# Attention in a four-stage kernel: scores of the next pair and values of the last pair alternate on the matmul engine

## The chip, the cores and the metric

The kernel runs on one core of a Trainium2 chip. A core has a matmul engine (PE, with its weight loads shown apart as PEld), three engines for other arithmetic (DVE, ACT, POOL), a queue that issues transfers (SP), and 16 DMA engines that all of them share. Each engine works through its own instructions in the order in which they were written; engines wait for each other by semaphores. The metric is the device time of one execution in microseconds (us), and what is compared are medians of several runs.

## The reference, cut to what matters

The model has four residual stages on `x` (32 sequences of 56 rows of 256), with `ctx` (32 x 1500 x 256) and a mask over the 1500 context rows. The change touches the third:

```python
x = x + _L0_xattn_ref(_layernorm(x), ctx, ...)      # a scan over ctx, summed
x = x + _L0_ffn_ref(_layernorm(x), ...)             # 16 experts, 6 of them a row
x = x + _L1_xattn_ref(_layernorm(x), ctx, mask)     # attention: the stage that is changed
x = x + _L1_ffn_ref(_layernorm(x), ...)             # 2 experts, the better one a row

def _L1_xattn_ref(hidden_states, memory_tokens, memory_mask):
    scale = 1.0 / jnp.sqrt(jnp.asarray(D, hidden_states.dtype))
    scores = jnp.einsum('bsd,bmd->bsm', hidden_states, memory_tokens) * scale
    scores = jnp.where(memory_mask[:, None, :], scores, -1e30)
    attn = jax.nn.softmax(scores, axis=-1)
    readout = jnp.einsum('bsm,bmd->bsd', attn, memory_tokens)
    return jnp.where(jnp.any(memory_mask, axis=-1)[:, None, None], readout, 0)
```

The context rows are keys and values at once. All is float32.

## The kernel before, in words

Two sequences make a **pair**: 16 pairs (`NP`), each 2 x 64 partitions of which 2 x 56 are real rows. `xr` holds the residual of all pairs in SBUF. The order of PE, DVE, ACT, SP and (in the attention stage) POOL is the order of the program text: `manual_schedule` keeps it, so "before" and "after" in the text are so on each engine's queue.

The attention loop runs `p` from 0 to 16. For each pair the work is:

- **Context.** A sequence's context is one slot of 128 x 12 x 256 float32 (1536 KB). There are 8 slots, five in `ring` and three `extra`; `load_ctx` (L145, SP) fills one. A pair's two slots are filled again, with the pair that comes four later, right after its values have been read (end of `attend`).
- **Keys turned.** `turn(p, n)` transposes half `n` of both sequences' contexts on DVE (`transposed`, L908, two instructions a half) into `cT`, four buffers: two halves of two sequences.
- **Scores.** `scores` (L947, PE, `sp`) goes over eight steps `e`, two sequences `h` and four strips `a`: 64 matmuls in the program, which the chip runs as 128 (each float32 matmul is two). Each uses 32 rows and 64 columns of the array, eight such tiles side by side. The four `sp` banks of PSUM have one buffer each.
- **Mask and softmax.** `masked` (L960, DVE) adds the mask terms `mf` and takes the maximum, from `sp` into `sc` (one buffer); `softmax` makes the bias `nb` (L970, DVE) and the exponentials in place (L972, ACT). `mask_added` (L930, ACT) writes `mf` for the next pair from `mu`, which `mask_terms` (L917, SP) loads.
- **Probabilities turned.** `turned` (L987, PE, and copies on ACT, L988) makes `pT`.
- **Values.** `attend` (L995, PE, `op`) sums 12 chunks for two sequences: 24 matmuls, 48 on the chip, each 128 rows by 64 columns, two side by side.
- **After that** `inverse` and `sort_rows` (L1029, DVE) scale and add the residual into `pay`; `stats1`, `roots`, `sort_norm`, `sort_gate` normalise the row and pick its expert; every fourth pair `sort_four`, `sort_rank` (PE, L1063) and `sort_place` compute where four pairs' rows go, and POOL scatters them to `xs1` in DRAM (L1086).
- **For a later pair:** `query_rows` (ACT, L735) and `queries` (PE, L754) prepare the queries of pair `p + 2`, and POOL gathers the second stage's results for pair `p + 5` (`results`, six gathers, L709) and adds them to `xr` (`added`, L719 to L722). This goes on to `p` = 10.

In iteration `p` PE's order is: scores of `p`, values of `p - 1` (held from the last iteration), queries of `p + 2`, a rank if there is one, probabilities of `p` turned. The softmax of `p` runs while PE does the values of `p - 1`. In the last iterations `order_of_blocks` (L1102, a small matmul) and `rows_of1` (L1133, POOL) start the fourth stage for the first `NY1` blocks; the weights of that stage (L1211, L1215, SP) go into `ring` slots 0 to 3, which the contexts of pairs 12 and 13 leave last. The fourth stage is `expert_blocks`: for each block of 128 rows `gate_up` (L647), `turn` and `down` (L674).

Of the kernel before, what the change touches and what calls it, by code (L numbers as in the profile page):

```python
# [8 lines left out]
F32 = mybir.dt.float32  # L9
# [9 lines left out]
P = 128  # L19
B, S, D, T = 32, 56, 256, 1500  # L20
KD = D // P
NP = B // 2
TOK = 2 * S
NM, JM = 3, 4
NCH = NM * JM
# [8 lines left out]
NQ1 = 4  # L34
# [6 lines left out]
NPG = E0 * CAP // P // 2  # L41
NL = CAP // P
NB0 = (B * S * K0 + E0 * (P - 1)) // P
NY1 = 3
NB1 = B * S // P + 1
WP = 2 * D + 2
EPS = 1e-5
# [7 lines left out]
def xattn_ffn_kernel(  # L55
# [23 lines left out]
    V, A, PE, G = nc.vector, nc.scalar, nc.tensor, nc.gpsimd  # L79
# [62 lines left out]
    slots = [ring[:, i, :].rearrange("p (j d) -> p j d", d=D) for i in range(NRING)]  # L142
# [62 lines left out]
    with tc.tile_pool(name="p1", bufs=1) as p1, tc.tile_pool(name="p3", bufs=3) as p3, tc.tile_pool(  # L205
        name="xn", bufs=4
    ) as xnp, tc.tile_pool(name="z", bufs=4) as zp, tc.tile_pool(name="p1_ps", bufs=6, space=PSUM) as ps, tc.tile_pool(
        name="p1_acc", bufs=2, space=PSUM
# [122 lines left out]
        for e in range(KD):  # L331
            PE.matmul(
                vp[:, 0:D], lhsT=bcol[:, e : e + 1].to_broadcast([P, P]), rhs=wout_sb[:, e, :],
                start=(e == 0), stop=False,
# [124 lines left out]
        def turned(p):  # L459
            keep(p, xT=turned_rows(p3, ps, "ps", pend[p]["xn"]))  # L460
# [419 lines left out]


    so = ctx.enter_context(tc.tile_pool(name="so", bufs=1))
    payp = ctx.enter_context(tc.tile_pool(name="pay", bufs=7))
    with tc.manual_schedule(
        engines={ET.PE, ET.DVE, ET.Activation, ET.SP, ET.Pool}
    ), tc.tile_pool(name="at", bufs=1) as at, tc.tile_pool(
# [27 lines left out]
        def mask_terms(p):  # L914

            mu = mus[p % 2]
            nc.sync.dma_start(  # L917
                out=mu, in_=bass.AP(mask.tensor, 2 * p * T, [[T, 2], [0, 64], [1, T]])
            )
            return mu  # L920
# [17 lines left out]
                AF.Identity, scale=BIG, bias=nbig,  # L938
            )

        def scores(cTs, xq):

            sps = [psc.tile([P, 512], F32, tag=f"sp{a}", name=f"sp{a}") for a in range(4)]
            for e in range(NE):
                for h in range(2):
                    for a in range(4):
                        PE.matmul(  # L947
                            sps[a][64 * h : 64 * h + 64, 0 : Q * NCH],
                            lhsT=xq[Q * a : Q * a + Q, e, 64 * h : 64 * h + 64],
                            rhs=cTs[e // 4][h][Q * a : Q * a + Q, :, e % 4, :],  # L950
                            start=(e == 0), stop=(e == NE - 1),
                        )
            return sps

        def masked(sps):
            sc = at.tile([P, NCH, P], F32, tag="sc", name="sc")
            mx = small.tile([P, 5], F32, tag="mx", name="mx")
            for a in range(4):
                cols = (slice(None), slice(None), slice(Q * a, Q * a + Q))
                V.tensor_tensor_reduce(  # L960
                    out=sc[cols], in0=sps[a][:, 0 : Q * NCH].rearrange("p (j q) -> p j q", q=Q),
                    in1=mf[cols], scale=1.0,
                    scalar=-3.0e38, op0=ALU.add, op1=ALU.max, accum_out=mx[:, a : a + 1],
                )
            V.tensor_reduce(mx[:, 4:5], mx[:, 0:4], AX.X, ALU.max)
            return sc, mx

        def softmax(sc, mx):
            nb = small.tile([P, 3], F32, tag="nb", name="nb")
            V.tensor_scalar(nb[:, 0:1], mx[:, 4:5], -ISC, None, ALU.mult)  # L970
            sf = sc.rearrange("p j q -> p (j q)")
            A.activation(sf, sf, AF.Exp, bias=nb[:, 0:1], scale=ISC, accum_out=nb[:, 1:2])  # L972
            return nb
# [14 lines left out]
                A.copy(pT[:, 4 * n : 4 * n + 4, :].rearrange("p j c -> p (j c)"), tp)  # L988
            return pT

        def attend(p, pT):
            op = po.tile([P, 512], F32, tag="op", name="op")
            for j in range(NCH):
                for h in range(2):
                    PE.matmul(  # L995
                        op[64 * h : 64 * h + 64, 0:D],
                        lhsT=pT[:, j, 64 * h : 64 * h + 64],
                        rhs=slots[(2 * p + h) % NS][:, j, :],
                        start=(j == 0), stop=(j == NCH - 1),
                    )  # L1000
            for b in (2 * p + NS, 2 * p + 1 + NS):
                if b < B:
                    load_ctx(b, slots[b % NS])
            return op


        GP = 4
# [19 lines left out]
        def sort_rows(p, op, nb):  # L1027
            pay[p] = payp.tile([P, WP], F32, tag="pay", name="pay")
            V.scalar_tensor_tensor(  # L1029
                pay[p][:, D : 2 * D], op[:, 0:D], nb[:, 2:3], xr[:, p, :], ALU.mult, ALU.add  # L1030
            )
            return stats1(pay[p][:, D : 2 * D])
# [107 lines left out]
        def turn(p, n):  # L1140
            return [transposed(2 * p + h, n) for h in range(2)]
# [5 lines left out]
        def results_until(p):  # L1147
            while sent[0] < due[min(p, NP - 1)]:
                results(*queue[sent[0]])
                sent[0] += 1  # L1150

        cTs = [turn(0, 0), turn(0, 1)]
        mask_added(mu_.pop(0))
        mvs, four = {}, []
        held = None
        for p in range(NP + 1):
            if p == NP - 1:
                order_of_blocks()

            if p + 2 < NP:  # L1160
                roots(mvq[p + 2])
            if p - 2 in mvs:
                roots(mvs[p - 2])
            if p + 2 < NP:
                xn = query_rows(p + 2, mvq.pop(p + 2))
                mu_[p + 2] = mask_terms(p + 2)
            if p - 2 in mvs:
                sort_norm(p - 2, mvs.pop(p - 2))
            if p < NP:
                sps = scores(cTs, xqs.pop(p))  # L1170
                if p + 1 < NP:
                    lo = turn(p + 1, 0)
                sc, mx = masked(sps)
                nb = softmax(sc, mx)
                if p + 1 < NP:
                    cTs = [lo, turn(p + 1, 1)]
                inverse(mx, nb)
            if held:
                op = attend(held[0], held[1])
                mvs[held[0]] = sort_rows(held[0], op, held[2])  # L1180
                held = None
            if NE0 <= p + NE0 < NP:
                added(p + NE0, [results(resp, p + NE0, NB0, i) for i in range(2)])
            if p + 3 < NP:
                mvq[p + 3] = stats1(xr[:, p + 3, :])
            if p + 2 < NP:
                xqs[p + 2] = queries(at2, ppt, "pt", xn, 0)
                queries(at2, ppt, "pt", xn, 1, xqs[p + 2])
            if four:
                sort_place(*four[0], sort_rank(four.pop()[1], ppt, "pt"))  # L1190
            if 0 <= p - 2 < NP:
                sort_gate(p - 2)
                if (p - 2) % GP == GP - 1:
                    o = p - 2 - GP + 1
                    four.append((o, sort_four(o)))
            if p < NP:
                held = (p, turned(sc), nb)
            if p + 1 < NP:
                mask_added(mu_.pop(p + 1))
            if p == NP - 1:  # L1200
                for i in range(NY1):
                    apart()
                    rows_of1(i, payp, "pay")
# [15 lines left out]
    with tc.tile_pool(name="f1", bufs=3) as wk, tc.tile_pool(  # L1219
        name="f1_tr", bufs=2, space=PSUM  # L1220
    ) as ptr, tc.tile_pool(name="f1_gu", bufs=2, space=PSUM) as pgu, tc.tile_pool(
        name="f1_ht", bufs=2, space=PSUM
    ) as pht, tc.tile_pool(name="f1_y", bufs=2, space=PSUM) as py:
        last = NP - GP

        def side1(t):

            if t == -1:
                roots(mvs[NP - 1])
                sort_norm(NP - 1, mvs.pop(NP - 1))  # L1230
                sort_gate(NP - 1)
                four.append((last, sort_four(last)))
            if t == 1:
                sort_place(*four[0], sort_rank(four.pop()[1], ptr, "tr"))
            if t == 2:
                experts_of_rest(ptr, "tr")
            i = t // NQ1 + 2
            if t % NQ1 == 1 and i >= NY1 and i < NB1:
                rows_of1(i, wk, "xb1")

        def done1(i, y):
            xb = xb1.pop(i)
            ti = wk.tile([P, 1], I32, tag="ti", name="ti")
            V.tensor_copy(ti, xb[:, WP - 1 : WP])
            ob = wk.tile([P, D], F32, tag="ob", name="ob")
            V.scalar_tensor_tensor(  # L1246
                ob, y[:, 0:D], xb[:, 2 * D : 2 * D + 1], xb[:, D : 2 * D], ALU.mult, ALU.add
            )
            loose("out", G.indirect_dma_start(  # L1249
                out=of, out_offset=bass.IndirectOffsetOnAxis(ap=ti[:, 0:1], axis=0),  # L1250
                in_=ob, in_offset=None, bounds_check=B * S - 1, oob_is_err=False,
            ))

        expert_blocks(
            NB1, NQ1, F1, w1_sb.rearrange("p e w -> p (e w)"), e1i,
            wk, ptr, pgu, pht, py, lambda i: xb1[i][:, 0:D], done1, 1, None, side1,
        )

# [55 lines left out]
```

## Time and profile before

| | us |
|---|---|
| median of 3 runs (lowest, highest) | 1027.94 (1022.82, 1030.45) |
| the profiled execution's own time | 1017.45 |
| its span, first to last instruction | 1015.7 |
| granted PE clock, mean | 0.882 |
| PE / PEld / DVE / ACT / POOL busy | 878.1 / 551.9 / 460.7 / 348.3 / 419.1 |
| attention stage (first scores to the fourth stage's first matmul) | 547.6 to 833.7 |

All times inside the execution count from the span's start. PE's busy time is no measure of its load: matmuls are pipelined, and the ends of matmuls are modelled. So the stage is read from the start of one group to the start of the next. In the tables of stretches each row has the stretch, its length, and for each engine its busy time with the number of instructions in brackets, then the granted PE clock (1.00 is full), the busy share of the DMA engines and the rate in GB/s. In the chain of waits and in the timeline each row has start, length, engine, line and what is written; in the timeline the bracket at the end is the engine's idle time just before, and what ended it ("issue": nothing that the profile shows).

### The profile page before, as it was taken

Reading aid. Unit: us, or ns where it says so; the run is one execution under the profiler, and the core shown is the slowest. Engines: PE = TensorE matmul, PEld = TensorE weight load, DVE = VectorE, ACT = ScalarE, POOL = GpSimd, SP = SyncE. Lnnn points to the kernel's source line nnn. Section 1 sums busy time; section 2 is a strip of 40 time slices with the busy share of each in tenths; the row PEclk is TensorE's granted clock in tenths of the full one; section 3 lists DMA queues with packets and bytes.
Section 4 is the critical chain, followed back from the end, with each engine's and each line's share of the span. In section 5 each row is a group of like instructions: output and inputs, shape, how many; then the busy total and the mean of one; then the engine's idle time right before and its main releaser. Section 6 shows DMA issues by size and latency. Waiting matters only on the chain.

```text
span 1015.7 us, 17756 instructions
## 1 busy us (share of the span) xinstructions
PE 878.1 (86%) x6122; PEld 551.9 (54%) x6122; DVE 460.7 (45%) x1447; ACT 348.3 (34%) x904; POOL 419.1 (41%) x487
## 2 busy tenths in 40 slices
PE   5687897761698989898898899899999999999997
PEld 4344443331476767676675456555556555666664
DVE  2565454534255323232225657655668933332332
ACT  0222221210242454543333464453466632111111
POOL 4155554544435555555542645644640023021111
PEclk9767655765799999999989799998899999999999
DMA  9999999999397633343435475675575472011110
GB/s 274 364 259 244 231 249 231 279 220 177 93 321 259 196 114 110 112 116 104 125 87 155 169 289 190 237 265 182 181 294 217 146 247 73 11 37 38 31 31 16
DMA packets 81145, 177.08 MB, mean 174 GB/s; under 512 B 10899, under 2 KB 44580, under 8 KB 81060
## 3 DMA queue, kind: packets, MB, share of 16 engines
q1 hardware_dynamic: 64884, 139.78, 45.3%
q0 software_dynamic: 16048, 35.95, 12.8%
q8 instruction: 52, 0.85, 0.4%
q14 instruction: 33, 0.27, 0.1%
q10 hardware_dynamic: 128, 0.23, 0.1%
HBM read 151.06 MB, written 25.53 MB: 174 GB/s over the span
## 4 chain that ended last, share of the span: by engine, by line
PE 64%; issue 6%; DMA 5%; DVE 3%; ACT 2%; another core or an unknown queue 1%; POOL 1%; ACTq 0%; SPq 0%; POOLq 0%; DVEq 0%
PE gu L647 20%; PE sp L947 13%; PE y L674 12%; PE op L995 8%; PE tp L665 3%; DMA ring<-in_cx 3%; PE tp L166 2%; PE tp L987 2%; PE tp L754 1%; DMA own<-pw,to 1%; DVE cT L908 1%; DMA w_sb<-in_wd 1%; ACT xT L168 0%; ACTq L787 0%
## 5 line engine op out<-in xcount | busy, mean ns | idle before, releaser
L647 PE MATMUL gu<-w_sb,xT 128*128 x396 | 139.6, 476 | 21.3 <-ACT xT L168 17.3
L947 PE MATMUL sp<-cT,xq 32*64 32x384 f32 x2048 | 141.5, 544 | 14.1 <-issue 10.6
L779 POOL DMA_INDIRECT xb<-xn,idx x99 | 94.7, 956 | 113.4 <-PE tp L166 89.6
L516 POOL DMA_INDIRECT own<-pw,to x96 | 95.8, 998 | 106.8 <-issue 94.9
L653 ACT ACTIVATE sg<-gu 128x176 f32<-128x176 f32 (+1 forms) x159 | 54.4, 343 | 219.6 <-PE gu L647 209.3
L659 DVE SCALAR_TENSOR_TENSOR hs<-sg,wgt,gu 128x176 f32<-128x176 f32 x99 | 39.3, 397 | 187.5 <-ACT sg L653 178.7
L647 PE MATMUL gu<-ring,xT 128*128 x240 | 114.3, 600 | 0.5 <-ACT xT L168 0.5
L947 PEld LDWEIGHTS sp<-cT,xq 32*64 32x64 f32 x2048 | 70.8, 147 | 76.3 <-issue 61.9
L709 POOL DMA_INDIRECT g<-ys,back x96 | 92.0, 958 | 34.4 <-issue 27.4
L647 PEld LDWEIGHTS gu<-w_sb,xT 128*128 128x128 f32 x396 | 75.4, 194 | 52.8 <-ACT xT L168 19.9
L674 PE MATMUL y<-w_sb,hT 88*128 x396 | 102.4, 381 | 0.0
L294 PE MATMUL acc<-ring,cz 128*32 128x256 f32 x768 | 79.1, 567 | 20.1 <-DMA ring<-in_cx 15.8
L908 DVE STREAM_TRANSPOSE cT<-ring 128x1536 f32<-128x1536 f32 x40 | 69.1, 1759 | 59.3 <-PE sp L947 32.9
L657 DVE TENSOR_TENSOR hs<-sg,gu 128x256 f32<-128x256 f32 x60 | 25.2, 421 | 117.1 <-ACT sg L653 117.1
L665 PEld LDWEIGHTS tp<-ident,hs 128*88 128x88 f32 (+1 forms) x318 | 41.6, 131 | 63.6 <-issue 49.6
L168 ACT COPY xT<-tp 128x256 f32<-128x256 f32 x130 | 48.4, 372 | 79.9 <-PE tp L166 66.1
L674 PEld LDWEIGHTS y<-w_sb,hT 88*128 88x128 f32 x396 | 68.0, 192 | 5.7 <-issue 0.2
L1249 POOL DMA_INDIRECT out<-ob,ti x15 | 15.0, 997 | 132.3 <-DVE ob L1246 121.7
L667 DVE COPY hT<-tp 88x256 f32<-88x256 f32 (+1 forms) x159 | 66.0, 415 | 2.1 <-PE y L674 1.4
L995 PE MATMUL op<-ring,pT 128*64 128x256 f32 x480 | 65.9, 384 | 0.0
L665 PE MATMUL tp<-ident,hs 128*88 128x128 f32 (+1 forms) x318 | 61.8, 277 | 2.6 <-DVE hs L657 2.6
L647 PEld LDWEIGHTS gu<-ring,xT 128*128 128x128 f32 x240 | 45.7, 191 | 33.1 <-issue 29.5
(264 smaller groups left out, 1274.4 us busy)
## 6 DMA issues: line engine op xcount, KB each, us to landing
ring<-in_cx SPq DMA_DIRECT2D x52, 1536.0 KB
extra<-in_cx SPq DMA_DIRECT2D x12, 1536.0 KB
ys<-yb SPq DMA_DIRECT2D x99, 128.0 KB
xs<-zrow SPq DMA_DIRECT2D x5, 771.0 KB
mu<-in_mask SPq DMA_DIRECT2D x16, 187.5 KB
w_sb<-in_wg SPq DMA_DIRECT2D x2, 1408.0 KB
w_sb<-in_wu SPq DMA_DIRECT2D x2, 1408.0 KB
xn<-xn SPq DMA_DIRECT2D x16, 128.0 KB
```

The costliest lines, as they stand in the source:

```text
L294: PE.matmul(acc[Q * g : Q * g + Q, 0:D], lhsT=cz[:, j, 1 - h : 1 - h + Q], rhs=c[:, j, :], start=(h == 0 and m == 0), stop=(h == 1 and m = ...
L516: loose("own", G.indirect_dma_start(out=own, out_offset=bass.IndirectOffsetOnAxis(ap=to[:, k : k + 1], axis=0), in_=pw[:, k, :], in_offset ...
L647: PE.matmul(gu[:, 0 : 2 * fp], lhsT=xT[i][:, k, :], rhs=w[:, bass.ds(at[i] + (u * piece + k * 2 * fp), 2 * fp)], start=(k == 0), stop=(k = ...
L653: A.activation(sg, gu[:, 0:fp], AF.Silu)
L665: PE.transpose(tp[0:h, c * P : (c + 1) * P], a[:, c * h : (c + 1) * h], ident)
L667: V.tensor_copy(hT[i, u], tp[0:h, 0 : 2 * P])
L674: PE.matmul(y[i][:, 0:D], lhsT=a[:, c * P : (c + 1) * P], rhs=w[0:h, bass.ds(at[i] + (u * piece + doff + c * D), D)], start=(u == 0 and c ...
L709: G.indirect_dma_start(out=g[:, k, :], out_offset=None, in_=ys0[0 : n * P, :], in_offset=bass.IndirectOffsetOnAxis(ap=back[:, p, 3 * i + k ...
L779: G.indirect_dma_start(out=xb, out_offset=None, in_=xn0, in_offset=bass.IndirectOffsetOnAxis(ap=idx[:, i : i + 1], axis=0),)
L908: V.transpose(out=cT.rearrange("p j e q -> p j (e q)"), in_=slots[b % NS][:, :, P * n : P * n + P],)
L947: PE.matmul(sps[a][64 * h : 64 * h + 64, 0 : Q * NCH], lhsT=xq[Q * a : Q * a + Q, e, 64 * h : 64 * h + 64], rhs=cTs[e // 4][h][Q * a : Q * ...
L995: PE.matmul(op[64 * h : 64 * h + 64, 0:D], lhsT=pT[:, j, 64 * h : 64 * h + 64], rhs=slots[(2 * p + h) % NS][:, j, :], start=(j == 0), stop ...
```

## The change

The scores go one more pair ahead. Scores and turned keys of pair 1 come before the loop; in iteration `p` PE computes scores of `p + 1` and values of `p - 1`, and the two are generators that `by_turns` takes one piece of each: after each of the eight steps `e` of the scores (8 matmuls in the program) come four or two matmuls of the values, by turns, so eight pieces of each. The probabilities of `p` are turned after that, from exponentials made at the end of the iteration before. `sc` has two buffers. The mask is loaded and added one pair earlier, too. `pay` has six buffers for seven, and two blocks of the fourth stage are fetched early for three; the third is fetched in its step 3.

```diff
-NY1 = 3
+NY1 = 2
...
-    payp = ctx.enter_context(tc.tile_pool(name="pay", bufs=7))
+    payp = ctx.enter_context(tc.tile_pool(name="pay", bufs=6))
...
-        def scores(cTs, xq):
-
-            sps = [psc.tile([P, 512], F32, tag=f"sp{a}", name=f"sp{a}") for a in range(4)]
+        def scores(cTs, xq, sps):
+
+            sps[:] = [psc.tile([P, 512], F32, tag=f"sp{a}", name=f"sp{a}") for a in range(4)]
             for e in range(NE):
...
-            return sps
+                yield
 
         def masked(sps):
-            sc = at.tile([P, NCH, P], F32, tag="sc", name="sc")
+            sc = at.tile([P, NCH, P], F32, tag="sc", bufs=2, name="sc")
...
-        def attend(p, pT):
-            op = po.tile([P, 512], F32, tag="op", name="op")
-            for j in range(NCH):
-                for h in range(2):
-                    PE.matmul(
...
+        def attend(p, pT, op):
+
+            for i in range(2 * NCH):
+                j, h = divmod(i, 2)
+                if i and i % 6 in (0, 4):
+                    yield
+                PE.matmul(
...
             for b in (2 * p + NS, 2 * p + 1 + NS):
                 if b < B:
                     load_ctx(b, slots[b % NS])
-            return op
+            yield
...
+        def by_turns(*parts):
+            parts = list(parts)
+            while parts:
+                parts = [g for g in parts if next(g, g) is not g]
+
         cTs = [turn(0, 0), turn(0, 1)]
         mask_added(mu_.pop(0))
-        mvs, four = {}, []
-        held = None
+        mu_[2] = mask_terms(2)
+        mvs, four, soft, held = {}, [], {}, {}
+        sps = []
+        by_turns(scores(cTs, xqs.pop(0), sps))
+        lo = turn(1, 0)
+        soft[0] = masked(sps)
+        soft[0] += (softmax(*soft[0]),)
+        cTs = [lo, turn(1, 1)]
+        mask_added(mu_.pop(1))
         for p in range(NP + 1):
...
-                mu_[p + 2] = mask_terms(p + 2)
+            if p + 3 < NP:
+                mu_[p + 3] = mask_terms(p + 3)
...
-            if p < NP:
-                sps = scores(cTs, xqs.pop(p))
-                if p + 1 < NP:
-                    lo = turn(p + 1, 0)
-                sc, mx = masked(sps)
-                nb = softmax(sc, mx)
-                if p + 1 < NP:
-                    cTs = [lo, turn(p + 1, 1)]
+
+            parts, sps = [], []
+            if p + 1 < NP:
+                parts.append(scores(cTs, xqs.pop(p + 1), sps))
+            if p >= 1:
+                op = po.tile([P, 512], F32, tag="op", name="op")
+                pT, mx, nb = held.pop(p - 1)
+                parts.append(attend(p - 1, pT, op))
+            by_turns(*parts)
+            if p + 1 < NP:
+                if p + 2 < NP:
+                    lo = turn(p + 2, 0)
+                soft[p + 1] = masked(sps)
+            if p >= 1:
                 inverse(mx, nb)
-            if held:
-                op = attend(held[0], held[1])
-                mvs[held[0]] = sort_rows(held[0], op, held[2])
-                held = None
+                mvs[p - 1] = sort_rows(p - 1, op, nb)
+            if p + 2 < NP:
+                cTs = [lo, turn(p + 2, 1)]
...
             if p < NP:
-                held = (p, turned(sc), nb)
+                sc, mx, nb = soft.pop(p)
+                held[p] = (turned(sc), mx, nb)
             if p + 1 < NP:
-                mask_added(mu_.pop(p + 1))
+                soft[p + 1] += (softmax(*soft[p + 1]),)
+            if p + 2 < NP:
+                mask_added(mu_.pop(p + 2))
...
+            if t == 3:
+                rows_of1(NY1, wk, "xb1")
             i = t // NQ1 + 2
-            if t % NQ1 == 1 and i >= NY1 and i < NB1:
+            if t % NQ1 == 1 and NY1 < i < NB1:
                 rows_of1(i, wk, "xb1")
```

More of the change, by code (lines that the diff above doesn't have):

```diff
@@ L989, in turned @@
             return pT
-        def attend(p, pT):
-            op = po.tile([P, 512], F32, tag="op", name="op")
-            for j in range(NCH):
-                for h in range(2):
[L995 to L1000, printed above, removed]
+        def attend(p, pT, op):
[4 more added lines that the diff above has]
+                PE.matmul(
+                    op[64 * h : 64 * h + 64, 0:D],
+                    lhsT=pT[:, j, 64 * h : 64 * h + 64],
+                    rhs=slots[(2 * p + h) % NS][:, j, :],
+                    start=(j == 0), stop=(j == NCH - 1),
+                )
             for b in (2 * p + NS, 2 * p + 1 + NS):
```

## The prediction, made before the changed kernel was run

> **What bounds the stage now.** I read the chain of waits first. In the late pairs it is PE alone, without a gap:
>
> ```profile
> 771.09 5.35 PE sp L947 x128
> 776.43 5.33 PE op L995 x48
> 781.76 1.03 PE tp L754 x8
> 782.79 1.38 PE tp L987 x12
> 784.17 5.35 PE sp L947 x128
> ```
>
> A pair costs 784.17 - 771.09 = 13.08 us: scores 5.35, values 5.33, small transposes 2.41. 16 pairs would take 210 us; the stage takes 286. The values always take 5.33 at full clock. What varies is the scores. Next I asked for the stretch of each pair's scores with the POOL gathers (L709) in it (columns: stretch, length, busy POOL us with its count, granted clock, DMA share, GB/s):
>
> ```profile
> 585.10:593.30 8.20, 1.96 (x3) 1.00 1.03 396
> 600.90:613.70 12.80, 3.77 (x4) 0.73 0.82 307
> 673.90:692.20 18.30, 5.80 (x6) 0.68 0.72 248
> 701.20:709.00 7.80, 1.66 (x2) 1.00 1.02 391
> 784.10:789.50 5.40, 0.00 (x0) 1.00 1.03 419
> sum 153.20, POOL 35.96; mean POOL 2.25
> ```
>
> The 16 stretches sum to 153.20 us where 16 x 5.40 = 86.4 would do: **66 us lost in the scores**, always where POOL issues gathers (or, for pairs 11 and 15, the scatters of L1086). Busy DMA alone does not do it: the last row has 1.03 and no loss. How it goes shows in stretches that begin where a burst of six gathers begins, and in those that follow (all engines; PE and its loads come first):
>
> ```profile
> 598.30:602.75 4.45, 4.45 (x62) 3.20 (x61) 3.68 (x12) 3.50 (x7) 3.53 (x4) 1.00 0.63 214
> 652.19:657.90 5.71, 5.71 (x67) 3.90 (x64) 5.18 (x16) 1.92 (x5) 4.49 (x5) 1.00 0.54 160
> 714.27:718.90 4.63, 4.63 (x63) 3.25 (x62) 3.14 (x12) 3.89 (x8) 3.71 (x4) 1.00 0.70 237
> ...
> 602.75:606.50 3.75, 2.78 (x12) 0.46 (x5) 0.00 (x0) 3.62 (x11) 2.22 (x3) 0.88 1.04 389
> 657.90:660.60 2.70, 1.26 (x8) 0.37 (x4) 1.04 (x6) 1.44 (x6) 1.26 (x2) 1.00 1.04 419
> ```
>
> From the burst's start PE gets through some 63 matmuls (55 to 70 in seven bursts), whatever they are, and then nearly stops (5 weight loads in 3.75 us) until about 1.2 us after the last gather (658.51 + 0.96, PE at pace again at 660.68). No semaphore is named: the releaser is "issue". So PE has a stock of some 63 matmuls and gets almost none while POOL writes gathers. Values use 24 matmuls (48 on the chip) in 5.33 us, and the stock outlasts the burst; scores use 24 a us, and it is gone in 2.6. A dry spell of 3.6 us or more is followed by half clock (0.73 in the rows above).
>
> ```profile
> 652.19 0.97 POOL L709 DMA_INDIRECT g<-ys,back  x1
> ...
> 658.51 0.96 POOL L709 DMA_INDIRECT g<-ys,back  x1 [0.30 <-issue]
> 665.35 1.83 POOL L719 TENSOR_TENSOR g<-g 128x768 f32<-128x768 f32 x1 [5.88 <-DMA g<-ys,back]
> ```
>
> A burst is 7.3 us long; with the wait for landing (5.9) and the additions (4.3) POOL goes round in some 17.7 us by itself, eleven times.
>
> **Part 1: changes between scores and values on PE.** The work of a pair is the same in number and size. But scores use tiles of 32x64, values of 128x64, and where one follows the other PE pauses:
>
> ```profile
> 775.59 0.85 PE L947 MATMUL sp<-cT,xq 32*64 32x384 f32 x16
> 776.37 0.87 PE L995 MATMUL op<-extra,pT 128*64 128x256 f32 x6
> ```
>
> Single starts: the last scores matmul at 775.954, the first of the values at 776.365, 0.411 us later where one tile's scores follow each other every 0.322; and the first pair of values lies 0.267 apart, later ones 0.2155. Lost: 0.089 + 0.052 = 0.14 us. Probabilities to scores (770.816 to 771.019) gives 0.144 in the same way, values to queries 0.155. Values to scores doesn't occur in this program; I take 0.14, the nearest rows, with 0 and 0.155 as ends. Eight pieces each make 15 changes where there was one, in the 14 iterations that have both (`p` 1 to 14): 14 x 14 x 0.14 = **+27.4 us** (0 to +30.4). Nothing lies beside it, as PE is the chain; nor can it be a gain, as scores and values each ran back to back before and left no gaps to fill. Scores and values of one iteration then take 10.68 + 1.96 = 12.64, a pair 15.05.
>
> The Trainium skill speaks against the change here: "TensorEngine Tiling (Array Packing)", Key Properties, says that changing the tiling mode, not just the tile, drains the engine. It gives no price; had PE overlapped the two modes, this term would be 0.
>
> **Part 2: the bursts.** Interleaved, PE uses 176 matmuls in 12.64 us, 13.9 a us. A burst of 7.3 + 1.2 = 8.5 us finds stock for 63 / 13.9 = 4.5, leaving some 4 dry, of which the trickle seen above gives back 0.5: 3.5 a burst, and as 4 is at the point where half clock followed (3.6 did, 2.7 did not), 0 to 2.5 more. Eight such bursts: 28 to 48. The first (scores of pair 0 are as before) 4.6, the second, over the small transposes, 3 to 4. The long one (four scatters and six gathers on end, 12.5 us; before, 12.9) 10 to 12.4. Four scatters alone, which let through more (19 matmuls in 3.8 us), 1.6, before 4.2. The last scatters meet no scores any more, before 3.6. Sum 47 to 70.6, mean 59, against 66: **-7 us** (-19 to +5).
>
> The skill would have this term at nothing: "Runtime: NRT & Kernel Launch", Instruction fetch mechanics, holds a kernel's instruction stream to be mostly hidden. The rows have PE short of instructions with no wait; where they stay the trace doesn't tell.
>
> **Part 3: the fourth stage's start.** Its weights go to slots that the values of pair 13 leave. These end at 807.87, and DMA stays busy (1.01) until 829, 0.57 to 831, then idle; the sequencer's waits before the first matmul (L647, 833.68) include the last weight load, which landed at 830.5, 22.7 us after. Before, scores of pair 15 (8.9 us) lay in that time, now they come ahead of it: PE is ready 25.8 - 8.9 = 16.9 after. It waits 5.8, or 7.6 with the sequencer's steps from landing to matmul: **+6 us** (0 to +7.6).
>
> **Part 4: small ones.** Before, PE waited 3.6 us in iteration 0 for the first softmax; now 2.3 for `masked` and up to 1 for a half turned: -1 (-3 to +3). In each iteration `masked` of `p + 1` now starts when its scores end, and PE's next scores, with the values queued behind them, wait for its four PSUM banks: 0.16 + 4 x 0.48 + 0.1 = 2.2 us, under 2.41 of small transposes. This covers it by 0.2; without, up to 2 an iteration. DVE then has 8.6 us of rows up to the bias `nb`, ACT 1.8 exponentials and 4.75 from mask to query rows: 15.1 after the values' end, just the new 15.05; with `sort_four` (1.9 on DVE) it is late by 2, in the one late iteration with it: **+2** (0 to +8). The mask's load is queued ahead of the context loads on SP and waits for ACT; that ends some 2 us before the values do. Transposing on DVE (3.43 a half) has 6.3 us of the other half's scores to hide in. `pay` with six buffers makes `sort_rows` wait for the first scatter of a group, an iteration (15 us) older. The third block's gather comes with those that ran at 850 and is needed at 856. Each of these is 0, and some 2 to 4 us once if the cover is gone, inside the ends above.
>
> **Sum:** 27.4 - 7 + 6 - 1 + 2 = +27.4. Against the profiled execution's own 1017.45 that is 1044.9. The median shown lies 10.5 higher, so the forecast for a median is 1027.94 + 27.4 = **1055 us**.
>
> **Rivals.** (a) *The stock lasts (faster).* The turns are there to thin PE's demand. The shortest stretch with a burst in it lost 2.4 us (701.20, 7.80 less 5.4). If each of ten bursts costs that, and the long one 9, scatters 1.6: 35, or -31; changes that fall into dry spells cost nothing, so half of them, 14; with +6 and +1, -10: 1018. If changes are at the low end, 0, it is 1004. It decides from 63 / (7.3 + 1.2 - 2.4) = 10.3 matmuls a us down; the turns need 13.9, which speaks against it. I put it at 1010. (b) *Changes cost little:* 0 to 5, with -7 for bursts and 0 to 7 for the rest: 1021 to 1033, say 1029. For it: weight loads are drawn ahead of matmuls within one shape. Against it: three measured changes agree on 0.14. That the turns don't reach PE at all is not likely, its order being the text's; the time would be this one. (c) *Context loads come late.* A pair's slots are filled after the values of `p - 1` and now turned in the middle of the next iteration, where they had one iteration more. Loads took 12.6 us (582.5 to 595.1) to 13.5 beside gathers, 10.4 to 11 without. With values ending at 12.64, second transpose 1.75 and masks 2.2, twice the period is at least 16.6 + landing: 15.0 at 13.5, not above 15.05. At 17 it is 16.8, 1.75 x 14 = +24.5 on the sum: 1080.
>
> **Numbers.** Forecast 0.55 (1040 to 1070); (a) 0.12; (b) 0.21; (c) 0.12. Range 1024 to 1080: it takes in most of (b), the forecast and half of (c), and leaves out (a). A measurement here tells about 1% from no change. Faster by over 1% (under 1017.7): (a), 0.12. Within 1% (to 1038.2): most of (b), 0.19. Slower: 0.69.
>
> **What would show it.** Late pairs (no POOL gathers) at some 15 us for 13.08, with 0.41 and not 0.32 us between a scores piece and the values after it; stretches of scores and values 12.6 without a burst, 16 to 19 with one; the first L647 later against the end of pair 13's values than 16.9. I am wrong if late pairs stay near 13 (changes are free), if the stretches with bursts stay under 14 (the stock lasts), or if DVE's transposes wait for loads (c).

## The result, and the profile after

| | before | changed |
|---|---|---|
| median (lowest, highest), four runs each | 1025.38 (1019.65, 1030.45) | 1078.7 (1070.36, 1085.61) |
| profiled execution, span | 1015.7 | 1077.7 |
| attention stage, first scores to first matmul of the fourth stage | 286.1 | 337.6 |
| second stage (its first L647 to the first scores), same code in both | 283.6 | 290.6 |

The change makes the kernel slower: ratio 1.0518, 95% interval 1.0421 to 1.0615, 53 us by the medians and 51.5 in the attention stage. The time of the kernel before differs between the batches in which experiments ran together (1025, 944.6, 944.5, 964.0, 1007.0 us), so below each kernel is set against the kernel before in its own batch, and stages against stages.

Stretches of scores and values in the changed kernel, six of the 14 (columns: stretch, length, busy POOL us in gathers with their count, granted clock, DMA share, GB/s):

```profile
607.60:627.30 19.70, 8.88 (x10) 0.83 0.56 212
...
693.20:715.00 21.80, 0.00 (x0) 0.84 0.39 150
...
762.20:778.10 15.90, 5.18 (x6) 1.00 0.66 250
782.00:802.90 20.90, 1.42 (x2) 0.84 0.42 157
...
838.80:851.90 13.10, 0.00 (x0) 1.00 0.59 234
854.30:875.40 21.10, 0.00 (x0) 0.84 0.17 54
```

Undisturbed they are 13.03 us (three of the 14, with clock 1.00, no gathers and no scatters), where scores and values took 10.68 before; the small transposes are still 2.41, so a late pair takes 15.44 for 13.08. Stretches with gathers are 16 to 20, and 22.7 where the scatters and six gathers come on end (718). And three are 21 to 22 us with few gathers or none: 693, 782 and 854, each the first after an iteration with `sort_four`. The last of them, in the timeline (start, length, engine, line, what; the bracket is the engine's idle time before, and what ended it):

```profile
851.51 0.56 DVE L960 CUSTOM_DVE_ANT_1 sc<-sp,mf 128x384 f32<-128x384 f32 x1 [1.44 <-PE sp L947]
...
854.27 0.90 PE L947 MATMUL sp<-cT,xq 32*64 32x384 f32 x16
855.34 3.43 DVE L908 STREAM_TRANSPOSE cT<-extra 128x1536 f32<-128x1536 f32 x2
859.52 0.16 DVE L1054 SCALAR_TENSOR_TENSOR w<-dd 128x4 f32<-128x4 f32 x1
859.71 0.21 ACT L1055 ACTIVATE w<-w 128x4 f32<-128x4 f32 x1 [6.08 <-DVE w L1054]
860.74 1.55 ACT L988 COPY pT<-tp 128x512 f32<-128x512 f32 x3
861.37 1.98 PE L997 MATMUL op<-ring,pT 128*64 128x256 f32 x8 [6.20 <-ACT pT L988]
```

The values need `pT`, which ACT copies. ACT works in the order of the text, and there the exponential of `sort_four` (L1055) stands ahead of those copies. It waits for DVE's `w`, and on DVE `w` is queued behind the masks, `sort_rows` and a half of turned keys (3.43 us), which start when the scores end. So ACT stands for 6.08 us, PE for 6.20, and at 0.84 of the clock the stretch loses 1.9 more: 8.07 over 13.03. The same wait was there before, 1.97 us long, and behind cover:

```profile
790.34 0.52 DVE L960 CUSTOM_DVE_ANT_1 sc<-sp,mf 128x384 f32<-128x384 f32 x1
...
797.19 4.13 PE L947 MATMUL sp<-cT,xq 32*64 32x384 f32 x96
798.34 0.15 DVE L1052 SCALAR_TENSOR_TENSOR w<-dd 128x4 f32<-128x4 f32 x1
798.52 0.20 ACT L1053 ACTIVATE w<-w 128x4 f32<-128x4 f32 x1 [1.97 <-DVE w L1052]
799.55 1.55 ACT L988 COPY pT<-tp 128x512 f32<-128x512 f32 x3
```

From the first mask to `w` DVE takes 8.0 us in both kernels (790.34 to 798.34, 851.51 to 859.52). But before, the masks started 4.4 us ahead of the end of the values (794.78), as those came after the scores; with the turns scores and values end together (851.86), and the masks start 0.35 us ahead of that. So `w` is 4.1 us later, as ACT's wait is.

Before, 5.35 us of scores lay between the turned probabilities and the values that need their copies; the copies were done at 801.1, the scores at 802.5. With the turns the first values come after one piece of scores, 0.83 us. So the turns work twice here: they make the copies later, and they take their cover.

### The profile page after: what moved, and what is told of

Read it like the earlier page. It is cut to its first block, busy times and chain, and to the rows that moved or that the text cites. A ratio compares the mean times of both kernels' runs of the same rounds, so it can differ in the third digit from the quotient of the medians.

```text
span 1077.7 us, 17757 instructions
## 1 busy us (share of the span) xinstructions
PE 910.8 (85%) x6122; PEld 523.6 (49%) x6122; DVE 462.7 (43%) x1447; ACT 347.9 (32%) x904; POOL 419.0 (39%) x486
## 4 chain that ended last, share of the span: by engine, by line
PE 60%; issue 5%; DVE 5%; ACT 3%; another core or an unknown queue 3%; DMA 1%; POOL 0%; ACTq 0%; POOLq 0%; DVEq 0%
PE gu L647 19%; PE y L674 12%; PE sp L947 11%; PE op L997 9%; PE tp L665 3%; PE tp L166 2%; DVE cT L908 2%; PE tp L987 1%; PE tp L754 1%; DVE sc L960 1%; ACT pT L988 0%; DMA xb<-xn,idx 0%; DVE st L154 0%; ACT xT L168 0%
## 5 line engine op out<-in xcount | busy, mean ns | idle before, releaser
L647 PE MATMUL gu<-w_sb,xT 128*128 x396 | 140.7, 479 | 23.4 <-ACT xT L168 18.2
L947 PE MATMUL sp<-cT,xq 32*64 32x384 f32 x2048 | 145.8, 551 | 9.0 <-issue 5.7
L647 PE MATMUL gu<-ring,xT 128*128 x240 | 112.9, 593 | 0.7 <-ACT xT L168 0.7
L997 PE MATMUL op<-ring,pT 128*64 128x256 f32 x480 | 90.1, 425 | 19.0 <-ACT pT L988 18.6
L674 PE MATMUL y<-w_sb,hT 88*128 x396 | 104.9, 389 | 0.0
L709 POOL DMA_INDIRECT g<-ys,back x96 | 92.1, 959 | 32.9 <-issue 27.1
L647 PEld LDWEIGHTS gu<-w_sb,xT 128*128 128x128 f32 x396 | 76.1, 196 | 55.0 <-ACT xT L168 20.9
L947 PEld LDWEIGHTS sp<-cT,xq 32*64 32x64 f32 x2048 | 42.4, 141 | 75.0 <-issue 68.0
L997 PEld LDWEIGHTS op<-ring,pT 128*64 128x64 f32 x480 | 35.7, 146 | 87.5 <-issue 54.5
L1088 POOL DMA_INDIRECT xs<-pay,to x16 | 15.9, 993 | 150.9 <-DVE nb L970 73.8
L960 DVE CUSTOM_DVE_ANT_1 sc<-sp,mf 128x384 f32<-128x384 f32 x64 | 31.8, 554 | 78.5 <-PE sp L947 56.4
```

The costliest lines, as they stand in the source:

```text
L647: PE.matmul(gu[:, 0 : 2 * fp], lhsT=xT[i][:, k, :], rhs=w[:, bass.ds(at[i] + (u * piece + k * 2 * fp), 2 * fp)], start=(k == 0), stop=(k = ...
L674: PE.matmul(y[i][:, 0:D], lhsT=a[:, c * P : (c + 1) * P], rhs=w[0:h, bass.ds(at[i] + (u * piece + doff + c * D), D)], start=(u == 0 and c ...
L709: G.indirect_dma_start(out=g[:, k, :], out_offset=None, in_=ys0[0 : n * P, :], in_offset=bass.IndirectOffsetOnAxis(ap=back[:, p, 3 * i + k ...
L947: PE.matmul(sps[a][64 * h : 64 * h + 64, 0 : Q * NCH], lhsT=xq[Q * a : Q * a + Q, e, 64 * h : 64 * h + 64], rhs=cTs[e // 4][h][Q * a : Q * ...
L997: PE.matmul(op[64 * h : 64 * h + 64, 0:D], lhsT=pT[:, j, 64 * h : 64 * h + 64], rhs=slots[(2 * p + h) % NS][:, j, :], start=(j == 0), stop ...
```

## The experiments

**Undo one part at a time.** The first experiment moves the turned probabilities ahead of the sort, so that ACT copies `pT` first:

```diff
+            if p < NP:
+                sc, mx, nb = soft.pop(p)
+                held[p] = (turned(sc), mx, nb)
             if four:
                 sort_place(*four[0], sort_rank(four.pop()[1], ppt, "pt"))
             ...
-            if p < NP:
-                sc, mx, nb = soft.pop(p)
-                held[p] = (turned(sc), mx, nb)
```

> The changed kernel with one edit: the probabilities of p are turned ahead of sort_place, sort_gate and sort_four in the program text, so ACT copies pT before it takes sort_four's exponential, which waits for DVE. Theory A (ACT's order: in three iterations the copies of pT wait 6 to 7 us behind that exponential, and PE falls to half clock after it): the stretches of scores and values after sort_four fall from 21.0-21.8 us to 13.0, or 16 where a burst of gathers lies in them; 3 x 8 = 24 us less, 1055 us. Theory B (those stretches are long by bursts of gathers and by the turns): no change, 1079 us.

The second has no turns; the third has both edits; the fourth makes the pieces twice as large:

```diff
-            by_turns(*parts)
+            for part in parts:
+                by_turns(part)
```

> The changed kernel without the turns: all scores of p+1 first, then all values of p-1; everything else as changed. Theory A (each change between the two costs PE 0.17 us): a late pair 13.1 us for 15.4, 14 x 2.35 = 33 us less; and as the scores end 5 us earlier, the transposes on DVE do too, and the wait behind sort_four's exponential shrinks by 5 us in three iterations: 1079 - 33 - 15 = 1031 us. Bursts then fall on scores alone and cost some 5 more: 1036. Theory B (changes cost little, waits make the loss): 1079 - 15 = 1064 us, late pairs at 15.

> Both edits: no turns, and probabilities turned ahead of the sort. Theory A: 1079 - 33 - 24 + 5 = 1027 us, within 1% of the kernel before, with late pairs at 13.1 us and no stretch after sort_four over 11 us without a burst. Theory B (a large part of the loss is in the earlier scores themselves, by bursts or late context loads): 1045 or more.

```diff
-                yield
+                if e % 2:
+                    yield
...
-                if i and i % 6 in (0, 4):
+                if i and i % 6 == 0:
```

> The changed kernel with pieces twice as large: two steps e of the scores, then six matmuls of the values; 7 changes an iteration for 15. Theory A (a price per change): undisturbed stretches 13.03 - 8 x 0.168 = 11.7 us, 14 x 1.34 = 19 us less: 1060 us. Theory B (the price is one of doing both at once, such as two shapes of weights drawn ahead, and not of the number of changes): 13.0 and 1079 us.

Since the kernel before was at 944.6 here, the changed kernel was run again in the next batch, beside a before of 944.5:

> The changed kernel itself, to have its time and profile beside the others: chips differ (the kernel before took 1025 us on the first and 944.6 on that of the four runs of single edits). If its loss is that of the first chip (ratio 1.052): 49 to 53 us over before. With it the single edits cost: turned first -22, no turns -25, half pieces -12. If the loss hangs on the chip's bursts, it is below 40.

It is 43.0 us over before, between the two ranges that were given for it.

| | median | ratio to before, 95% | attention stage | against changed |
|---|---|---|---|---|
| changed, again | 987.5 | 1.0448 (1.0381 to 1.0516) | 291.7 | |
| probabilities ahead of the sort | 971.6 | 1.0290 (1.0239 to 1.0341) | 274.8 | -15.9 |
| no turns | 968.3 | 1.0266 (1.0198 to 1.0335) | 272.6 | -19.2 |
| both | 969.9 | 1.0267 (1.0226 to 1.0308) | 272.2 | -17.6 |
| half as many pieces | 981.1 | 1.0395 (1.0347 to 1.0442) | 281.8 | -6.4 |

Each edit does to its own stretches what was expected. With the probabilities ahead, the three stretches after `sort_four` fall from 22.11, 21.53 and 21.69 to 14.22, 13.87 and 13.03, together 24 us, so without ACT's order the loss is gone. Without the turns, and with ACT's order as it was, it nearly goes too: PE waits 2.0 us in all for those copies, where it waited 20.1 in the changed kernel of the next batch (first row; total us, times, longest). The loss takes both.

```profile
PE op L997 <- ACT pT L988: 20.1, 3, 7.0
```

```profile
PE op L997 <- ACT pT L988: 2.0, 3, 0.9
```

Without turns the undisturbed stretch is 10.68 again. With half as many pieces it is 11.69: six changes more than the one of before cost 1.01, fourteen more cost 2.35, and both are 0.168 us a change, the mean of the two directions:

```profile
637.80:649.50 11.70, 11.70 (x178) 5.46 (x177) 8.78 (x18) 7.32 (x16) 5.50 (x9) 1.00 0.77 301
```

(a stretch of that kernel, with busy time and count on PE, PEld, DVE, ACT and POOL). But the times gain less than expected (24, 43, 52 and 19 us), and the two edits together gain no more than one. Something else takes over. In the two kernels without turns PE now waits for turned keys, 15.7 and 18.5 us in all. In the first experiment one place shows it: a new stretch of 23.08 us at 711, with these rows.

```profile
719.25 0.48 DVE L1031 SCALAR_TENSOR_TENSOR pay<-op,nb,xr 128x256 f32<-128x256 f32 x1 [6.64 <-DMA xs<-pay,to]
719.83 1.98 PE L997 MATMUL op<-extra,pT 128*64 128x256 f32 x8 [6.74 <-issue]
```

`sort_rows` waits for a scatter from the `pay` buffer that it wants to write, which POOL had issued late, behind its gathers; and the next values, as `op` has one buffer, start 0.1 us after `sort_rows` ends (the row itself names no releaser). That the sixth buffer alone is to blame isn't shown: no run has these edits with seven, and the kernel before, with seven, has one such wait in its later profile (7.1 us on DVE, 2.5 on PE).

**Without gathers.** To see the order of work alone, three kernels leave the second stage's results for pairs 5 to 15 out of the residual:

```diff
-            if NE0 <= p + NE0 < NP:
-                added(p + NE0, [results(resp, p + NE0, NB0, i) for i in range(2)])
```

> The kernel before without the POOL gathers and additions of the second stage's results for pairs 5 to 15 (it leaves that part of the residual out). Theory A (66 us of the scores are lost to bursts of gathers): 66 us less than before on a chip like the first; where a burst takes 2 to 4 us, as in the stretches of the four single edits (13.2 to 14.8 us for 10.7), 25 to 35 less. Theory B (bursts only fill time in which PE would wait for something else, such as a context load): less than 15 us less; stretches of scores and values longer than 10.7 us remain.

> The changed kernel with the same part left out. The bursts' cost in it is the difference to the changed kernel; the prediction has 59 us for before's 66, that is 7 less. Theory A: its stretches are 13.0 us except the three after sort_four at 21; against before without gathers it is 14 x 2.35 + 3 x 8 = 57 us slower less some 3 at the start. Theory B (bursts and waits overlap): under 45 us slower than before without gathers.

> The changed kernel without turns and with the probabilities turned ahead of the sort, and with the same part left out. With the gathers it was 25 us slower than before. Theory A (that rest comes from POOL: scatters that come late hold DVE in sort_rows, as pay has six buffers, and bursts now fall on scores that run on end at the start): within 5 us of before without gathers. Theory B (it is the order of scores a pair ahead itself: DVE's rows and the tail): 20 us or more over before without gathers.

| without gathers | median (before 944.5) | attention stage |
|---|---|---|
| before | 915.6 | 222.7 |
| changed | 984.9 | 285.7 |
| changed, no turns, probabilities ahead | 951.4 | 251.4 |

In the kernel before, every stretch of scores and values is now 10.68. In the changed one they are 13.03, but for three. The wait of PE that matters there (total us, times, longest), and three stretches (after the engines: clock, DMA share, GB/s):

```profile
PE op L997 <- ACT pT L988: 20.1, 3, 6.9
```

```profile
593.60:606.60 13.00, 13.00 (x177) 4.59 (x176) 9.33 (x15) 7.56 (x17) 0.00 (x0) 1.00 0.62 242
609.00:631.90 22.90, 15.95 (x177) 5.25 (x176) 10.68 (x24) 8.75 (x23) 0.00 (x0) 0.78 0.37 143
...
753.60:775.50 21.90, 15.71 (x177) 5.15 (x176) 6.48 (x19) 7.04 (x19) 0.00 (x0) 0.84 0.18 54
```

No gathers lie in them; PE's next longest wait in the stage sums to 2.8. The 63.0 us between the two stages (285.7 - 222.7) are 14 x 2.35 = 32.9 for the changes, 9.84 + 9.50 + 8.92 = 28.3 for the stretches after `sort_four`, and 1.8 that remain for start and end. By the medians the two are 69 apart; the rest lies outside the stage. Theory A held in its kind, and is 9 us short in the stage (57 less 3 were expected): with no burst at all the change costs more than in the result.

For the third kernel theory A fell: it is 28.7 slower in the stage than before without gathers, with stretches of 11.7 to 14.8 in 11 of 14. Its chain of waits (start, length, what) goes round through the loads:

```profile
610.95 5.38 PE op L997 x48
...
616.77 13.20 DMA ring<-in_cx
...
631.77 0.52 DVE sc L960
...
635.64 3.36 DVE cT L908 x2
639.04 2.81 PE sp L947 x56
641.85 5.38 PE op L997 x48
```

A slot is loaded for 13 us after its values, then transposed, behind that DVE masks the last scores, turns the other half, and only then PE can go on. To separate the load from DVE's rows, the next kernel reads old contexts:

```diff
-            for b in (2 * p + NS, 2 * p + 1 + NS):
-                if b < B:
-                    load_ctx(b, slots[b % NS])
             yield
```

> The kernel without turns, probabilities ahead of the sort and no gathers (951 us), and in it no slot is filled again: contexts of pairs 4 to 15 are left out, those of pairs 0 to 3 are read again in their place. Theory A (with the scores a pair further ahead, the load of a slot lies in a ring with the transposes, the mask and the scores, and that ring sets its pace where the turns no longer do): 915 to 925 us, stretches of 10.7 us throughout, as in before without gathers. Theory B (DVE's rows in their new order hold the scores): 940 us or more, stretches of 11.7 to 14.8 stay.

It took 947.1 us beside a before of 964.0; its first stage was 21.6 longer than that of the kernel with loads (265.4 to 243.8), where the two programs are the same. By its median theory B would hold; without those 21.6 us it is at 925.5, the end of theory A's range. So the attention stages are compared: 229.3 for 251.4, and all stretches but three within 0.01 of 10.68. DVE's first wait in the two, with loads and without:

```profile
DVE cT L908 <- DMA ring<-in_cx: 26.8, 13, 4.0
```

```profile
DVE pay L1028 <- PE op L997: 16.5, 12, 4.1
```

So 22 of the 28.7 us were the loads; the other 6.6 were not taken apart. Scores one more pair ahead means contexts turned one pair earlier, and at 13.1 us a pair the load is not there in time. The turns hid that by making the pair 15.4.

**What gathers cost.** Leaving them out gained 28.9 us in the kernel before and 2.7 in the changed one. Two runs of the kernel before look for the reason, one as it is and one with its gathers spread:

> The kernel before itself, one look, for its profile on the chip of the experiments. Leaving out the gathers gained 29 us there and 2.7 in the changed kernel. Theory A (PE is short of instructions while POOL writes gathers, and less so on this chip): stretches of scores and values with a burst are 2 to 4 us over 10.68, late pairs stay at 13.08, and the matmuls that start within a burst of 7.3 us are more than the 63 of the first chip. Theory B (the 29 us are in the wait for POOL's additions or in context loads): those stretches are near 10.7 and the small transposes longer than 2.41.

```diff
+    def added_by_ones(pool, p):
+
+        for u in range(K0 * p, K0 * p + K0):
+            if u == K0 * NE0:
+                for v in range(6):
+                    ones_[u + v] = one(pool, u + v)
+            G.tensor_tensor(xr[:, p, :], xr[:, p, :], ones_.pop(u), ALU.add)
+            if u + 6 < K0 * NP:
+                ones_[u + 6] = one(pool, u + 6)
...
-                added(p + NE0, [results(resp, p + NE0, NB0, i) for i in range(2)])
+                added_by_ones(resp, p + NE0)
```

(`one` is a single gather into one of six tiles.)

> The kernel before with the six gathers of a pair no longer on end: six tiles of one gather each, and by turns one addition to the residual and the gather that takes the freed tile, for pairs 5 to 15. The same gathers, six short additions for four. If the length of a burst makes the loss (PE's stock lasts through one gather of 1.2 us and is filled up during the 0.7 of an addition): most of the 29 us come back, 920 to 930 us. If each gather costs PE the same wherever it stands: 944, no change. As POOL no longer waits for a landing, pairs are ready earlier, which gains nothing by itself.

The kernel before took 961.6 us in that profile, with 249.1 in the attention stage. Two whole bursts in it; the first number in brackets is the count of PE's matmuls:

```profile
600.20:607.40 7.20, 7.20 (x147) 3.91 (x147) 5.10 (x11) 6.09 (x16) 5.67 (x6) 1.00 0.73 226
691.50:698.70 7.20, 7.01 (x132) 4.67 (x137) 6.63 (x19) 6.56 (x18) 5.68 (x6) 1.00 0.58 178
```

and one of the profile before the change, in the same view:

```profile
714.30:721.50 7.20, 6.39 (x68) 3.66 (x67) 3.11 (x12) 6.36 (x16) 5.67 (x6) 1.00 0.82 298
```

The same six gathers, 68 matmuls in one execution, 132 and 147 in the other. (Not every burst of the later profile shows it so plainly: where values lie in one, which use 9 matmuls a us, some 50 start. In the earlier profile 61 to 70 start in ten of the eleven bursts, whatever lies in them.) PE's shortage during gathers, on which the prediction built 66 us, is a condition of the execution and not of the kernel. Where it is absent the stretches are at or near 10.7 and the small transposes longer, as theory B said: gathers then delay the context loads. DVE waits 20.5 us for loads in the stage, in nine places, and PE 17.7 for exponentials, in seven; without gathers DVE doesn't wait for loads, and PE 3.3 us, once.

```profile
671.28 1.78 DVE L908 STREAM_TRANSPOSE cT<-extra 128x1536 f32<-128x1536 f32 x1 [4.45 <-DMA extra<-in_cx]
675.36 1.57 ACT L972 ACTIVATE sc<-sc,nb 128x1536 f32<-128x1536 f32 x1 [9.60 <-DVE nb L970]
677.08 2.82 PE L987 MATMUL tp<-ident,sc 128*128 128x128 f32 x12 [5.56 <-ACT sc L972]
```

This is one of the seven: a late load, a late transpose, a mask behind it on DVE, a late exponential, PE waiting. Spreading the gathers then gains little: 958.7 us, ratio 0.9938 (0.9906 to 0.9970), stage 243.7 for 249.1. That is neither the 20 us of the one theory nor the nothing of the other.

**The two repairs together.** The last kernel is the changed one with the probabilities ahead of the sort and with spread gathers.

> The changed kernel with the probabilities turned ahead of the sort (1.029 of before), and with the gathers of pairs 5 to 15 taken one by one between additions, as in the kernel before with the same edit (0.994 of before). With the turned probabilities ahead, one stretch of scores and values was new and long, 23 us for 13: DVE stood 6.6 us in sort_rows for a scatter that POOL had issued late, behind its gathers and their landing. Theory A (POOL's round of 17 us is longer than the pair of 15.4 and falls behind): without the wait for landings the round is 12 us, the scatter comes in time, that stretch falls to 13 to 14, and the time to 1.015 to 1.020 of before; what then stays is the price of the changes, 33 us less what the kernel before loses by gathers. Theory B (the scatter's own path, the six buffers alone, makes it late): the long stretch stays, 1.025 or more.

It took 986.4 us against 1007.0, ratio 0.9817 (0.9741 to 0.9893), and the stretch of 23.08 is 13.04, as theory A said. Neither theory had the time. This batch was one of those in which PE is held up: its second stage took 287.9 us, as in the two profiles of the result (283.6 and 290.6), where all other experiments show 264.6 to 270.3. Its attention stage is 270.3, against 286.1 in the profile of the kernel before under that condition, and its stretches with gathers are 13.0 to 15.0 us, not 16 to 20 (POOL's column counts the gathers alone):

```profile
571.40:584.40 13.00, 6.39 (x7) 1.00 0.87 318
605.40:618.50 13.10, 6.60 (x7) 1.00 0.93 321
```

So it beats the kernel before in a batch where PE is held up. Elsewhere it probably would not: before's stage is 249.1 there, and this order of work with the gathers on end takes 274.8, of which the stretch of 23.08 is 10. But it wasn't run there, nor was the kernel before with spread gathers run where PE is held up, so which edit made the 1.8% is open.

## Why the prediction was right or wrong

The side was right, and 1078.7 lies in the range of 1024 to 1080, by 1.3 us. That it does is luck: the upper end stood for rival (c), late context loads, which did not come, and what filled the range in their place, a loss behind `sort_four`, no rival held. The sum of +27.4 met 51.5 in the stage.

**Part 1** held in its mechanism. The term of 14 x 14 x 0.14 = 27.4 was mis-sized: 14 x 14 x 0.168 = 32.9, above its upper end of 30.4. The price came out low in the reading of the prediction's own rows: the 0.411 us from the last scores matmul to the first of the values was set against 0.322, which is the step from one tile's scores to the next of the same tile. From the last of the eight tiles to the first of the next eight it is 0.276 (775.631 to 775.907). So that change costs 0.135 + 0.052 = 0.187. In the changed kernel the step is again 0.410; a piece of scores takes 0.83 for 0.644 (2 x 0.322) and one of four pairs of values 1.015 for 0.862 (4 x 0.2155), 0.19 and 0.15 over, with a mean near 0.168. A late pair is 15.44 for the 15.05 forecast. Rival (b), changes at little cost, is out: the price is the same 0.168 with 7 and with 15 changes. What the Trainium skill says in "TensorEngine Tiling (Array Packing)", Key Properties, that a change of tiling mode drains the engine, agrees with a price per change.

**Part 2**, -7: leaving the gathers out gives 286.1 - 222.7 = 63.4 for what they cost before, 337.6 - 285.7 = 51.9 after, so -11.5. This compares profiles of held-up executions with profiles of others, and is rough for that. In the later batches the same difference is 249.1 - 222.7 = 26.4 and 291.7 - 285.7 = 6.0, -20.4. This fits the loads: in the later profile of the kernel before, late ones cost PE 17.7 us of waits for exponentials; in that of the changed kernel, with a pair at 15.4, DVE waits 27.0 us for loads, but PE waits for no exponential. The stock of 63 matmuls was read rightly and taken for a property of the kernel. What the skill says in "Runtime: NRT & Kernel Launch", Instruction fetch mechanics, that the instruction stream is mostly hidden, fits the later batches; whether PE's dry spells in the result's executions are late instructions no run shows, as the rows name no releaser. Rival (a), that the stock lasts, failed in the result's runs, where stretches with bursts were 16 to 20 us. In the batch of the changed kernel's second run it came nearer (13.0 to 14.8, but for two that follow `sort_four`), and the kernel was slower all the same, 1.0448 of before: the loss behind `sort_four` was missing in (a), too.

**Part 3** had the size for another reason. The first L647 came at 897.44, 22.07 after pair 13's values ended (875.37), 5.2 over the 16.9 of a PE that is not kept; +6 was forecast. But it was no wait for weights. DMA in 40 slices of 0.95 us from 862:

```profile
DMA  0000000000599999999999999999999613583000
```

The weights are in by 894, while PE does the last values until 896.3. What kept PE stands on DVE:

```profile
888.86 0.48 DVE L1031 SCALAR_TENSOR_TENSOR pay<-op,nb,xr 128x256 f32<-128x256 f32 x1 [6.05 <-DMA xs<-pay,to]
```

```profile
889.45 6.93 PE L997 MATMUL op<-extra,pT 128*64 128x256 f32 x48 [2.56 <-issue]
```

`sort_rows` of pair 14 waits for a scatter from the `pay` buffer that it writes, issued only from 880.29 on, and the last values, which need the one `op` buffer that it reads, start 0.11 us after it ends. The row of PE names no releaser, so this link is read from the program. From the probabilities to the values it is 4.09 us for 1.46 before, and the values run in part at half clock, 6.86 for 5.33: 2.6 + 1.5 of the 5.2. The rest lies around the probabilities ahead of pair 14's values (4.66 for 3.88) and at the start.

**Part 4** is the step that failed: "with `sort_four` (1.9 on DVE) it is late by 2, in the one late iteration with it: +2 (0 to +8)". Measured: 8.78 + 7.93 + 8.07 = 24.8 us over 13.03, in three iterations. That line counted DVE and ACT up to the query rows `xn`, one user of ACT, and not the copies of `pT` that stand in ACT's queue behind the same exponential and that PE needs soonest. Nor did it ask for the cover of those copies, which was the 5.35 us of scores that the turns cut to 0.83; and the late iteration with the sort is not the only one to pay: those that end at 693 and 782 pay as much, with few gathers or none behind them. Of the rest, the small transposes stayed at 2.41. The sentence that puts `pay` with six buffers at 0, or 2 to 4 us once, holds the other miss: it is what stands in Part 3's place, with 4.1.

**Rival (c)**, late context loads, was rightly put at a period that 15.05 just covers: in the result's profile of the changed kernel DVE waits 4.8 us in all for loads to `extra`, in the later one 27.0 for all loads, and PE waits for turned keys 2.5 and 2.8. Without the turns it is what sets the pace.

So the 51.5 are 63.0 (32.9 changes, 28.3 behind `sort_four`, 1.8 the rest, all measured without gathers) less 11.5 for gathers, which is what remains and has no measurement of its own.

## What to carry to other kernels

When two pieces of work are interleaved, list for every piece what it waits for and what used to lie in front of it: the copies of `pT` were free behind 5.35 us of scores and cost 8 us behind 0.83. List as well what waits for its end: the masks came 4 us later, as the scores ended with the values. On each engine that works in order, look at what is queued ahead of the instruction that the critical engine needs next, and put small side work (here the sort) behind it. An order that runs one pair further ahead needs its inputs one pair earlier; a slowdown elsewhere can hide that this is missing, and undoing the slowdown then gains nothing.

## What the runs showed of the hardware

A change between matmuls on 32x64 and on 128x64 tiles costs PE 0.168 us on the mean of both directions, the same with 7 and 15 changes a pair. In a wait of PE of 6.20 us (from 855.17 in the changed kernel) the granted clock fell to half at 858.46, 3.3 us into it, and stayed there for 6.83 us, 3.9 of them after PE had work again (0.84 over the stretch of 21). And whether PE starves while POOL issues six gathers differs between executions of one program: 68 matmuls in 7.2 us in one, 132 and 147 in another, with the second stage, whose code is the same in all these kernels, at 284 to 291 or 265 to 270 us. What sets the condition the runs don't tell.
